# Every fourth partition: a block exchange of an attention and expert kernel laid out anew

## The chip, the cores and the metric

The kernel runs on one core of a Trainium2 chip. Its time is the device time of one launch in microseconds (us), from the start to the end of the program on that core; the figure to be compared is the median of several launches. All engines are named as in the profile: PE is TensorE (its weight loads are listed as PEld), DVE is VectorE, ACT is ScalarE, POOL is GpSimd, and SP is SyncE, which here only issues DMAs.

## What is computed

Sixteen sequences of 256 tokens with 256 features each go through an attention block and then, all 4096 tokens together, through a mixture of eight experts. All numbers are float32. Cut to what matters:

```python
h   = _ln(x, ln1_g, ln1_b) + silu(t) @ W_ada.T + b_ada
qkv = (h @ Wqkv.T).reshape(b, n, 3, H, HD)                 # H = 16 heads, HD = 64
q   = _ln(qkv[:, :, 0].transpose(0, 2, 1, 3), qn_g, qn_b)  # norm over HD
k   = _ln(qkv[:, :, 1].transpose(0, 2, 1, 3), kn_g, kn_b)
v   = qkv[:, :, 2].transpose(0, 2, 1, 3)
attn = softmax(einsum('bhnd,bhmd->bhnm', q, k) / sqrt(HD))
o   = einsum('bhnm,bhmd->bhnd', attn, v)
x   = x + o.transpose(0, 2, 1, 3).reshape(b, n, H * HD) @ Wout.T
tok = x.reshape(-1, d)
vals, idx = top_k(softmax(tok @ Wgate.T).T, bs // E)       # each expert takes 512 tokens
# then per expert: norm, fc1, gelu, fc2, times vals, added back to tok[idx]
```

The sum over a head's 64 columns, of which the norms of q and k need the mean and the squares, does not depend on the order of these columns. Neither does the product of q and k, as long as both have the same order. That is what the change makes use of.

## The kernel before

**Stages.** A short start loads weights and norms the first sequence. Then 16 sequences pass through attention, overlapped with each other; the trace has their norms' evictions (line 659) on average 47 us apart. From about 750 us on the last sequence, the choice of the experts' tokens and then 16 expert jobs follow (8 experts, in two halves), to the end at 1089.5 us.

**Order.** The kernel writes its own order. Every piece of work is a step with an engine and a place in time (`Plan`, line 45); the places are a fixed list of numbers (`PLACES`, line 182), sorted once. So each engine has a fixed queue, worked off in order, and an instruction that waits holds up all that stand behind it on its engine. The same holds for SP, whose queue of DMA issues is worked off in order too.

**One sequence.** For each of six groups of 512 columns of the weights `wq` (two for q, two for k, two for v) and each of the two halves of 128 tokens, `Group.matmul` (line 688) makes `pm`, 128 tokens by 512 columns, in PSUM. For q and k, ACT squares it (701), DVE sums the squares over each head (705), POOL makes the inverse root (711, 103), and DVE scales `pm` into `qk` in SBUF (721). The mean has been taken out of the weights beforehand, once (`center`, 600).

q and k are needed with the head's columns on partitions. For the first and the last sequence (`DIRECT`, line 171), TensorE turns them (730). For the other 14 the turn is an *exchange* in two parts. DVE's transpose (754) turns blocks of 32 by 32: afterwards partition 32k + d holds column d of a block for the tokens of block k. Then the four block rows have to change places with the four quarters of partitions, and that is done by DMA: `away` (761) stores all 128 partitions into a DRAM buffer `blocks[k, d, q, n]` (512 KB), and `back` (773) reads it with four loads of 128 KB, one for each quarter q of the columns, each into 32 partitions. ACT then applies gain and bias (`affine`, 781 and 789).

The softmax takes the same way. `Quad.scores` (813) puts scores of 128 tokens by 256 keys into PSUM banks (tile `sc`, four of them), DVE takes the maxima (821), ACT the exponentials with their sums (830, tile `pr`), DVE the inverse (837), POOL normalises (841), DVE turns 32 by 32 blocks (851), SP stores (859) and loads with four DMAs (873), and `product` (900) multiplies with v. `evict` (915), the output projection (926) and the routing's gate (963) end a sequence.

**Buffers that couple the engines.** `pm` and other small products share three PSUM banks of the tag `mm`; `sc` has four banks; `pb` (the turned blocks) three buffers, the DRAM blocks four, `prT` four.

Before the change, the load of quarter q writes the 32 partitions from 32q on. The order of the keys in the scores' columns is (block k, half t, m), and the exponentials are taken over 256 columns that lie side by side.

## Time and profile before

| What | Value |
|---|---|
| three runs | 1093.52, 1088.24, 1091.94 us |
| median | 1091.94 us |
| the profiled execution: its own time | 1091.3 us |
| its span, first to last instruction | 1089.5 us |
| granted TensorE clock, mean of the span | 0.993 |
| DMAs of the exchanges | 168 stores of 512 KB, 672 loads of 128 KB |
| all DMA traffic | 238.56 MB, of it 100.66 MB written to HBM |

The profile is a page and a trace of one execution. Its groups give, for all instructions of a line with the same operands, the count, the time in which any of them ran (busy), the mean duration of one in ns, and how long the engine stood idle just before them, with what ended that idle time. The table of stages gives the busy time of each engine in a stretch of the span, the granted clock, the mean busy share of the 16 DMA engines and the rate they moved. The table of waits names who waited, for whom, the total in us, how often and the longest wait. A busy TensorE need not be one at its peak, since the ends of matmuls are modelled; the distance from one start to the next is the firmer measure.

### The profile page before, as it was taken

Reading aid. Unit: us, or ns where it says so; the run is one execution under the profiler, and the core shown is the slowest. Engines: PE = TensorE matmul, PEld = TensorE weight load, DVE = VectorE, ACT = ScalarE, POOL = GpSimd, SP = SyncE. Lnnn points to the kernel's source line nnn. Section 1 sums busy time; section 2 is a strip of 40 time slices with the busy share of each in tenths; the row PEclk is TensorE's granted clock in tenths of the full one; section 3 lists DMA queues with packets and bytes.
Section 4 is the critical chain, followed back from the end, with each engine's and each line's share of the span. In section 5 each row is a group of like instructions: output and inputs, shape, how many; then the busy total and the mean of one; then the engine's idle time right before and its main releaser. Section 6 shows DMA issues by size and latency. Waiting matters only on the chain. (4 is left out here: it accounts for less than half of the span.)

```text
span 1089.5 us, 18716 instructions
## 1 busy us (share of the span) xinstructions
PE 1050.4 (96%) x5611; PEld 686.6 (63%) x5611; DVE 809.4 (74%) x2257; ACT 592.3 (54%) x1656; POOL 617.5 (57%) x997
## 2 busy tenths in 40 slices
PE   6999999999999999999999999999988999999996
PEld 4555646555454655555565555656667888888885
DVE  6658888889788797898888887885678588655440
ACT  1768666666566665675666656675612322332331
POOL 3676776778667686667757666665501333333332
PEclk9999999999999999999999999999999999999998
DMA  6025899999999999998999999985130556655661
GB/s 214 1 78 165 269 276 304 291 281 257 283 292 280 280 299 290 289 280 263 277 299 286 265 302 265 321 260 164 61 102 20 149 161 199 186 171 163 192 203 20
DMA packets 167700, 238.56 MB, mean 219 GB/s; under 512 B 17328, under 2 KB 139440, under 8 KB 167600
## 3 DMA queue, kind: packets, MB, share of 16 engines
q1 hardware_dynamic: 159680, 227.08, 69.9%
q0 software_dynamic: 6144, 8.39, 4.2%
q10 hardware_dynamic: 1776, 1.90, 0.5%
q8 instruction: 45, 0.74, 0.3%
q14 instruction: 55, 0.45, 0.1%
HBM read 136.64 MB, written 100.66 MB: 218 GB/s over the span
## 5 line engine op out<-in xcount | busy, mean ns | idle before, releaser
L688 PE MATMUL pm<-wq,hT 128*128 128x512 f32 x768 | 362.1, 607 | 10.1 <-DVE qk L721 3.9
L841 POOL TENSOR_SCALAR pr<-pr,sums 128x256 f32<-128x256 f32 x512 | 237.6, 485 | 102.6 <-DVE sums L837 95.0
L830 ACT ACTIVATE pr<-sc,nmax 128x256 f32<-128x256 f32 x512 | 237.7, 482 | 92.3 <-DVE nmax L821 75.2
L688 PEld LDWEIGHTS pm<-wq,hT 128*128 128x128 f32 x768 | 137.1, 191 | 165.3 <-issue 131.3
L103 POOL TENSOR_TENSOR ss<-ss,neghalf 128x8 f32<-128x8 f32 x128 | 211.2, 1650 | 10.7
L821 DVE TENSOR_REDUCE nmax<-sc 128x2 f32<-128x512 f32 x256 | 165.3, 672 | 19.4 <-PE sc L813 19.1
L851 DVE STREAM_TRANSPOSE pb<-pr 128x512 f32<-128x512 f32 x224 | 150.0, 689 | 15.9 <-POOL pr L841 9.4
L813 PE MATMUL sc<-kT,qT 64*128 64x256 f32 x1024 | 136.8, 396 | 1.0 <-ACT kT L789 0.6
L701 ACT ACTIVATE sq<-pm 128x512 f32<-128x512 f32 x128 | 76.4, 605 | 102.5 <-PE pm L688 100.5
L900 PE MATMUL po<-prT,v 128*64 128x256 f32 x1024 | 129.0, 387 | 1.3 <-DMA prT<-blocks 1.3
L813 PEld LDWEIGHTS sc<-kT,qT 64*128 64x128 f32 x1024 | 91.3, 186 | 50.3 <-issue 28.9
L1319 POOL DMA_INDIRECT out<-y,idx x32 | 51.3, 1604 | 120.6 <-DVE y L1313 66.0
L1286 PE MATMUL ph<-xT,w 128*128 128x256 f32 x512 | 117.8, 383 | 0.0
L1302 PE MATMUL py<-w,hid 128*128 128x256 f32 x512 | 116.3, 380 | 0.0
L926 PE MATMUL pw<-wo,oT 128*128 128x256 f32 x512 | 115.3, 382 | 0.0
L926 PEld LDWEIGHTS pw<-wo,oT 128*128 128x128 f32 x512 | 96.2, 190 | 20.9 <-issue 6.0
L830 ACT ACTIVATION_READ_ACCUMULATOR pr<-sc,nmax 128x1 f32 x512 | 109.2, 213 | 0.0
L900 PEld LDWEIGHTS po<-prT,v 128*64 128x64 f32 x1024 | 66.5, 136 | 66.0 <-issue 20.1
L705 DVE TENSOR_REDUCE ss<-sq 128x8 f32<-128x512 f32 x128 | 85.0, 669 | 28.8 <-ACT sq L701 28.3
L1293 ACT ACTIVATE hid<-ph,vec 128x256 f32<-128x256 f32 x128 | 60.4, 474 | 84.4 <-PE ph L1286 79.4
L1302 PEld LDWEIGHTS py<-w,hid 128*128 128x128 f32 x512 | 95.6, 190 | 12.8
L1286 PEld LDWEIGHTS ph<-xT,w 128*128 128x128 f32 x512 | 95.4, 190 | 12.8
(141 smaller groups left out, 1098.3 us busy)
## 6 DMA issues: line engine op xcount, KB each, us to landing
blocks<-pb SPq DMA_DIRECT2D x112, 512.0 KB, 4.7
prT<-blocks SPq DMA_DIRECT2D x448, 128.0 KB, 4.1
kblocks<-kb SPq DMA_DIRECT2D x56, 512.0 KB, 4.1
w<-in_fc2T SPq DMA_DIRECT2D x16, 1024.0 KB, 5.8
w<-in_fc1T SPq DMA_DIRECT2D x16, 1024.0 KB, 8.3
qraw<-kblocks SPq DMA_DIRECT2D x112, 128.0 KB, 4.0
kT<-kblocks SPq DMA_DIRECT2D x112, 128.0 KB, 4.1
out<-tok SPq DMA_DIRECT2D x32, 128.0 KB, 3.9
```

The lines of the kernel that those rows point to most:

```text
L103: nc.gpsimd.tensor_tensor(dst, src, neghalf[:, : src.shape[1]], ALU.pow)
L688: nc.tensor.matmul(self.pm, hTs[self.b][:, c, bass.ts(self.t, P)], wq[:, c, bass.ts(self.g, GW)], start=(c == 0), stop=(c == DC - 1),)
L705: nc.vector.tensor_reduce(self.ss[:, 0, :], self.sq.rearrange("p (h d) -> p h d", d=HD), AX.X, ALU.add,)
L813: nc.tensor.matmul(self.sc[i, j][:, t, :], qTs[self.b][rows, hp, bass.ts(t, P)], keys[rows, hp] if direct else keys[rows, hp // 4, hp % 4] ...
L821: nc.vector.tensor_reduce(self.nmax[i, j], self.sc[i, j], AX.X, ALU.max, negate=True)
L830: nc.scalar.activation(self.pr[i, j][:, t, :], self.sc[i, j][:, t, :], AF.Exp, bias=self.nmax[i, j][:, t : t + 1], scale=1.0, accum_out=se ...
L841: nc.gpsimd.tensor_scalar(self.pr[i, j][:, t, :], self.pr[i, j][:, t, :], self.sums[i][:, 1, j, t : t + 1], 1.0, ALU.mult, ALU.mult,)
L851: nc.vector.transpose(self.pb[i][:, :, :, j].rearrange("p k c t n -> p t k c n"), self.pr[i, j].rearrange("p t (k c m) -> p t k c m", c=TB ...
L900: nc.tensor.matmul(self.po[j * HD : (j + 1) * HD, i, :], vs[self.b][:, c, bass.ts(4 * self.d + 2 * i + j, HD)], prT[:, j, c] if self.b in ...
L926: nc.tensor.matmul(self.pw, oTs[self.b][:, hp // 2, self.t, hp % 2, :], wo[:, hp, :], start=(hp == 0), stop=(hp == HP - 1),)
L1286: nc.tensor.matmul(self.ph[f], self.w1[:, c, bass.ts(f, P)], self.xT[:, c, :], start=(c == 0), stop=(c == DC - 1),)
L1302: nc.tensor.matmul(self.py[i], self.hid[:, f, bass.ts(i, P)], self.w2[:, f, :], start=(f == 0), stop=(f == FC - 1),)
```

## The change

The 32 partitions that a load writes are no longer neighbours: the load of quarter q writes the partitions q, q + 4, q + 8 and so on. For that, column 4d + q of a pair of heads has to stand at place d of quarter q. The weights for q and k are therefore laid out on the host by quarter: a group's 512 columns stand as (quarter, head, 16 columns) where they stood as (head, 64 columns). All that goes by head on these columns (centering, sum of squares, scaling) now walks four runs of 16 columns for each head.

For the softmax the keys of the scores are now in their natural order, and the exponentials read each fourth column of PSUM and write 64 of them side by side, quarter after quarter. For the two sequences without an exchange, the scaling writes `qk` in the original order of columns, each element four elements from the last. The centering becomes three instructions where it was two.

```diff
         def center(g, c):
-            w3 = wq[:, c, bass.ts(g, GW)].rearrange("p (h d) -> p h d", d=HD)
+            w3 = wq[:, c, bass.ts(g, GW)].rearrange("p (q e d) -> p q e d", q=QB, e=8)
             ws = stat.tile([P, 8], F32, tag="ws", bufs=2, name="ws")
-            nc.vector.tensor_reduce(ws, w3, AX.X, ALU.add)
-            nc.vector.scalar_tensor_tensor(
-                w3, ws.unsqueeze(2).to_broadcast([P, 8, HD]), -1.0 / HD, w3, ALU.mult, ALU.add
-            )
+            nc.vector.tensor_reduce(ws, w3.rearrange("p q e d -> p e q d"), AX.XY, ALU.add)
+            nc.vector.tensor_scalar_mul(ws, ws, -1.0 / HD)
+            nc.vector.tensor_tensor(w3, w3, by_head(ws), ALU.add)
+
+        def by_head(x):
+            return x.unsqueeze(1).unsqueeze(3).to_broadcast([P, QB, 8, HD // QB])
...
                 nc.vector.tensor_reduce(
-                    self.ss[:, 0, :], self.sq.rearrange("p (h d) -> p h d", d=HD),
-                    AX.X, ALU.add,
+                    self.ss[:, 0, :], self.sq.rearrange("p (q e d) -> p e q d", q=QB, e=8),
+                    AX.XY, ALU.add,
                 )
...
+                if self.b in DIRECT:
+                    dst = self.qk.rearrange("p (e d q) -> p q e d", q=QB, e=8)
+                else:
+                    dst = self.qk.rearrange("p (q e d) -> p q e d", q=QB, e=8)
                 engine.tensor_tensor(
-                    self.qk.rearrange("p (h d) -> p h d", d=HD),
-                    src.rearrange("p (h d) -> p h d", d=HD),
-                    self.ss[:, 1, :].unsqueeze(2).to_broadcast([P, 8, HD]), ALU.mult,
+                    dst, src.rearrange("p (q e d) -> p q e d", q=QB, e=8),
+                    by_head(self.ss[:, 1, :]), ALU.mult,
                 )
...
                 nc.vector.transpose(
                     kb[0][:, :, self.t],
-                    self.qk.rearrange("p (h q d) -> p q h d", q=QB, d=SQ),
+                    self.qk.rearrange("p (q h d) -> p q h d", q=QB, d=SQ),
                 )
...
                     nc.sync.dma_start(
-                        raw[bass.ts(q, SQ)], self.blocks[:, :, q].rearrange("k d n -> d k n")
+                        raw[q::QB], self.blocks[:, :, q].rearrange("k d n -> d k n")
                     )
...
                 keys = plain(kTs[self.b]) if direct else (
-                    kTs[self.b].rearrange("p g k t h m -> p g h (k t) m")
+                    kTs[self.b].rearrange("p g k t h m -> p g h t k m")
                 )
...
                 for t in range(TB):
+                    dst, src = self.pr[i, j][:, t, :], self.sc[i, j][:, t, :]
+                    if not (self.b in DIRECT):
+                        dst = dst.rearrange("p (q c m) -> p q c m", q=QB, c=TB)
+                        src = src.rearrange("p (c m q) -> p q c m", q=QB, c=TB)
                     nc.scalar.activation(
-                        self.pr[i, j][:, t, :], self.sc[i, j][:, t, :], AF.Exp,
+                        dst, src, AF.Exp,
...
                     nc.sync.dma_start(
-                        prT[bass.ts(q, SQ)], self.blocks[i][:, :, q].rearrange("k m n -> m k n")
+                        prT[q::QB], self.blocks[i][:, :, q].rearrange("k m n -> m k n")
                     )
...
+    qk = a["Wqkv"][: 2 * H * HD].reshape(-1, 8, HD // 4, 4, D).transpose(0, 3, 1, 2, 4)
...
-        "wqkvT": a["Wqkv"].T,
+        "wqkvT": np.concatenate([qk.reshape(-1, D), a["Wqkv"][2 * H * HD :]]).T,
```

Each engine's queue has the same instructions in the same order as before, apart from eight small multiplications on DVE, one for each centering. The number of DMAs, their sizes and their order in SP's queue are the same.

## The prediction

> **What bounds the kernel now.** I read the engines' shares first, then the stages, the waits and the groups of the lines that the change touches. The page's busy lines, the stages of the exchange (75 to 735 us) and of the expert jobs (850 to 1080 us; columns: time, then PE, PEld, DVE, ACT and POOL busy with instructions, granted clock, DMA share, GB/s):

> ```profile
> PE 1050.4 (96%) x5611; PEld 686.6 (63%) x5611; DVE 809.4 (74%) x2257; ACT 592.3 (54%) x1656; POOL 617.5 (57%) x997
> DMA  6025899999999999998999999985130556655661
> ...
> 75.00:735.00 660.00, 650.80 (x3156) 368.00 (x3154) 553.40 (x1099) 435.66 (x1286) 456.81 (x786) 1.00 0.96 277
> 850.00:1080.00 230.00, 229.64 (x1486) 201.03 (x1484) 134.63 (x731) 73.65 (x151) 77.32 (x64) 1.00 0.58 170
> ```

> TensorE is the bound: 650.8 of 660 us in the exchange stage, at full clock. Since its ends are modelled I also took the distances between starts: a matmul of the groups starts 429 ns after the last in the median, scores 108 ns on average in the first sequence and in the exchanged ones alike, the projection 216 ns. These are the same at all times. Adding up what is beyond the usual distance for each pair of lines gives 24.7 us of real stalls between 60 and 800 us, and 14 us in the first 50. No more than these can be won by anything that leaves TensorE's work alone. Beside it the 16 DMA engines are 96% busy in the exchange stage (277 GB/s), DVE 84% (553.4 of 660), ACT 66%.

> Who waits for DMAs, and for DVE:

> ```profile
> ACT kT L789 <- DMA kT<-kblocks: 12.3, 13, 1.9
> DVE st L615 <- DMA xs<-in_x: 11.5, 6, 4.0
> ACT qT L781 <- DMA qraw<-kblocks: 8.9, 8, 3.0
> DVE pb L851 <- DMA kblocks<-kb: 5.0, 6, 2.0
> PE pm L688 <- DVE qk L721: 3.9, 4, 2.9
> ```

> (Waiter, what for, total us, times, longest.) The loads of the softmax's exchange hardly appear: the products start 6.3 us (median) after their operands have landed, and only one stalled, for 1.25 us. The DMAs are full, but TensorE mostly doesn't feel it.

> **The change part by part.**

> *Loads onto every fourth partition.* 672 loads of 128 KB; number, bytes and SP's issues stay. In the trace, the 79,650 packets of 1 KB between 150 and 700 us, three quarters of them of these loads, take 66.9 ns on average: 45% take 45 to 50 ns, 38% 70 to 110. In the expert stage such packets take 51.6 ns. If the slow ones are those that share a way into SBUF, and spreading them makes all like the expert stage's, the engines save 15.3 ns x 79,650 / 16 = 76 us each of 550: their share falls from 0.98 to 0.84, and loads land earlier than today's 4.0 to 4.1 us. What reaches TensorE is only what it now loses behind a DMA: I followed the larger stalls back and find five, of 1.42 (149.7 us, product on its own load), 1.48 (279.3, behind DVE's wait for `xs`), 0.62 (406.9), 0.85 (472.4) and 0.89 us (658.8), the last three behind ACT's waits for `kT` and `qraw`. The rest is hidden. That is 5.3 us; as some will only shrink I take **-5.0**. Bounds: 0, and all stalls, -24.7.

> [...]

> *Exponentials read each fourth column* (16 bytes apart), 448 of the 512:

> ```profile
> L830 ACT ACTIVATE pr<-sc,nmax 128x256 f32<-128x256 f32 x512 | 237.7, 482 | 92.3 <-DVE nmax L821 75.2 <-POOL pr L841 7.8 <-POOL ss L103 4.8
> L1172 DVE TENSOR_SCALAR partf<-pplace 128x256 f32<-128x256 f32 x2 | 0.8, 424 | 4.1 <-PE pplace L1161 4.1
> ...
> L998 DVE TENSOR_TENSOR gate_of<-gates,smax 128x224 f32<-128x224 f32 x1 | 0.8, 765 | 0.0
> L990 DVE TENSOR_TENSOR gates<-gates,smax 128x224 f32<-128x224 f32 x1 | 0.4, 391 | 0.0
> ```

> No row shows ACT or PSUM with such steps. L998 writes SBUF in steps of 128 bytes, L990 does the same work in a row: (765 - 391) / 224 = 1.67 ns more an element. L1172 writes in steps of 8 bytes: 424 ns, as much as rows of 256 elements written in a row take (411 to 424, L627), so free; L1173 beside it also reads so, at 422. So an exponential costs between +0 and 256 x 1.67 = +428 ns. It is a read in steps of 16 bytes, nearest to L1173's read: I take **0**. Priced as a rival below.

> [...]

> *Scaling.* 128 instructions of 512 elements, 678 ns (L721). 112 read and write in a row as before: 0. The 16 of the first and last sequence write in steps of 16 bytes: 0 to 512 x 1.67 = 855 ns each. Between 8 and 128 bytes neither row is near, so I take half, 0.43 us. In the first sequence TensorE waits for these very instructions (the 3.9 us above, 2.9 of them at 24 us), so eight count: **+3.4** (0 to +6.8). Those of the last lie in DVE's idle 16%; without that cover, 3.4 to 6.8 more.

> *Centering.* One tiny instruction more for each of eight: L837's 128x4 takes 157 ns and is the nearest, so 0.16 us each. The first two are hidden by the 2.0 us for which DVE then waits for the next weights; five lie between that and the scaling at 23.4 us for which TensorE waits: **+0.8**. Nothing hidden would be 1.3.

> *Sums of squares* read runs of 16 elements: L705 takes 669 ns with runs of 64 for each head, the maxima (L821) 672 with runs of 256. Run length shows no price; 0. *Turns:* L754 (four rows of runs) 695 ns, L851 (all in a row) 689: 112 x 6 ns = 0.7 us of DVE, hidden in its idle time. *Keys in natural order:* scores take 108 ns with keys in a row (first sequence) and in runs of 32 (the others); still runs of 32: 0. Weights laid out on the host cost the chip nothing.

> *Sum.* The profiled execution took 1091.3 us (span 1089.5 and 1.8 around it; the median of the runs is 0.6 above). 1091.3 - 5.0 + 3.4 + 0.8 = **1090.5 us**: no change that can be told. A measurement of this kernel tells about 0.5% (5.5 us) from none.

> **The rivals.**

> A, the sum above: reads are free, and the queue's relief is small. Bounds with its own terms: 1083 (twice the DMA's gain, scaling free) to 1097 (scaling at full price and some of it in the last sequence). Chance 0.43.

> B, slower: **the stepped read of PSUM costs ACT.** At the middle, +214 ns, a sequence's 32 exponentials add 6.8 us to ACT's 31 of every 47 us. I pushed each exponential in the trace back by that, let ACT's idle time take up what it can, and compared with the time that TensorE's waits on ACT had to spare (a new score finds its bank free 3 us early in the median, 1.0 in the tightest tenth): 41 waits come late, and the latest in each 6 us add up to 19 us. So 1110 us. It decides early: 4 us at +100 ns, 9 at +150, 44 at +300, 154 at +428. Squares that come late also keep DVE and the banks of `mm`, which is not in it. For it: L998; against it: L1172, and that L998 is a write. Chance 0.35, mostly 1097 to 1135.

> C, faster: **the full DMA queue is behind more stalls than I could follow** (DVE's and SP's waits for stores, slow issues). Half of the 24.7 us goes: 1091.3 - 12.4 + 0.8 = 1079.7 us. Against it: the 6.3 us that products have to spare. Chance 0.11.

> D, **the loads get no faster**, because the packets are slow for another reason (stores and loads mixed, HBM): then only costs are left, 1091.3 + 3.4 + 0.8 = 1095.5 us. For it: the spread of the packets between 70 and 110 ns isn't one sharp peak. Chance 0.11.

> **How the numbers follow.** The likeliest is A with 1090.5 us. Faster by over 0.5% (below 1086.5): 0.13 of A and C's 0.11, 0.24. Within: 0.26 of A, 0.08 of D, 0.02 of B, 0.36. Slower (above 1097.4): 0.33 of B, 0.04 of A, 0.03 of D, 0.40. For 8 in 10 the range reaches from C's value, 1079, to the better part of B, 1125; A alone would be 1083 to 1097.

> **What will show it.** The exponentials' mean: 482 ns, or 600 and more. The mean of the 1 KB packets, near 52 or still 67, and the DMA share of the exchange stage, 0.84 or 0.96. The waits of ACT for `kT` and `qraw` should halve. The sixteen scalings in steps, at 678 or up to 1530 ns. The stalls of TensorE in the exchange stage, 20 us or fewer under A, about 45 under B. I am wrong if an exponential costs 100 ns more, or if the stalls nearly vanish with the DMA's load.

## The result, and the profile after

The changed kernel takes 1128.82 us in the median of four runs (1125.81 to 1130.98); the kernel before, beside it on the same chip, 1090.55 us (four runs, 1088.24 to 1093.52). The ratio is 1.0347, with a 95% interval of 1.0307 to 1.0388: it is slower, and lies above the predicted range. The profiled execution has a span of 1124.0 us, against 1089.5.

First the same lines of the page and the stages as before (busy engines, DMA share in 40 slices; then time, PE, PEld, DVE, ACT, POOL busy, clock, DMA share, GB/s):

```profile
PE 1062.0 (94%) x5611; PEld 691.8 (62%) x5611; DVE 816.3 (73%) x2265; ACT 592.4 (53%) x1656; POOL 615.7 (55%) x997
DMA  6024878887877788787888877777221366566661
...
75.00:735.00 660.00, 631.57 (x3014) 356.73 (x3013) 531.59 (x1058) 413.49 (x1219) 437.97 (x756) 0.99 0.79 264
850.00:1080.00 230.00, 225.84 (x1517) 197.79 (x1516) 152.28 (x828) 72.82 (x153) 73.89 (x63) 0.99 0.54 159
```

In the exchange stage the DMA share is down from 0.96 to 0.79, and TensorE starts 3014 matmuls where it started 3156. The stage has 660 us, so TensorE is idle for 28 of them (660 - 631.57), where it was for 9. Less load on the DMAs came with less work done by all engines: 264 GB/s, where it was 277.

Who waits for DMAs, and for DVE (waiter, what for, total us, times, longest):

```profile
DVE st L617 <- DMA xs<-in_x: 19.2, 8, 5.4
DVE pb L860 <- DMA kblocks<-kb: 17.0, 11, 3.3
ACT qT L786 <- DMA qraw<-kblocks: 16.2, 10, 4.8
ACT kT L794 <- DMA kT<-kblocks: 14.2, 13, 2.0
PE pm L690 <- DVE qk L727: 9.6, 8, 3.9
```

Every one has grown: the waits for `qraw` from 8.9 us, for `kT` from 12.3, for a `pb` buffer that a store still holds from 5.0, for `xs` from 11.5, TensorE's for the scalings from 3.9. Yet the packets, the pieces of which a transfer consists, are not slower. Those of 1 KB between 150 and 700 us take 54.2 ns on average (66.9 before), 90% of them under 50. And the exponentials, the prediction's main fear, cost what they did (482 ns before):

```profile
L839 ACT ACTIVATE pr<-sc,nmax 128x256 f32<-128x256 f32 x512 | 237.1, 480 | 106.5 <-DVE nmax L826 84.9 <-POOL pr L850 9.9 <-PE po L909 4.9
```

What had changed is in the detail of one line, the loads of the softmax's exchange. The columns are the engine, the operation and its count, then the time that issuing one keeps SP busy (shortest/median/longest in ns), and the first and last start in us; the rest isn't used here. Before:

```profile
L873 SPq DMA_DIRECT2D prT<-blocks x448: 302/430/2175, 97.3 to 748.8; - x150
```

After:

```profile
L882 SPq DMA_DIRECT2D prT<-blocks x448: 577/602/1706, 100.0 to 781.8; - x150
```

A load onto every fourth partition takes SP 602 ns to issue instead of 430, and never less than 577. The loads of q and k show the same. The last one is issued 33.0 us later than before, which is nearly all of the 34.5 us by which the span grew. Summed over the exchange stage, SP is busy issuing DMAs for 523 us of 660, where it was 410. SP's own waits fit this: an engine that comes later finds more of what it waits for done. Before and then after, its waits for the softmax's stores to land (total us, times, longest):

```profile
SPq L873 <- DMA blocks<-pb: 63.4, 44, 5.5
```

```profile
SPq L882 <- DMA blocks<-pb: 29.3, 21, 3.6
```

The loads differ in the program as built, too. Every DMA that SP and ACT issue in the kernel before carries a mark, 979 in all. In the changed kernel 307 carry it; the 672 without it are the stepped loads. It is called the mark for a short issue here, since the loads of the kernel before, with nothing else changed, took 599 ns to issue without it (run 3). The trace agrees: in it SP's stores are still issued in 319 ns at the least, the stepped loads never under 577.

### The profile page after: what moved, and what is told of

Same layout as the page of the kernel before. It is cut to its first block, busy times and chain, and to the rows that moved or that the text cites. A ratio compares the mean times of both kernels' runs of the same rounds, so it can differ in the third digit from the quotient of the medians.

```text
span 1124.0 us, 18753 instructions
## 1 busy us (share of the span) xinstructions
PE 1062.0 (94%) x5611; PEld 691.8 (62%) x5611; DVE 816.3 (73%) x2265; ACT 592.4 (53%) x1656; POOL 615.7 (55%) x997
## 5 line engine op out<-in xcount | busy, mean ns | idle before, releaser
L690 PE MATMUL pm<-wq,hT 128*128 128x512 f32 x768 | 368.5, 616 | 16.7 <-DVE qk L727 9.6
L690 PEld LDWEIGHTS pm<-wq,hT 128*128 128x128 f32 x768 | 139.7, 194 | 174.4 <-issue 141.0
L103 POOL TENSOR_TENSOR ss<-ss,neghalf 128x8 f32<-128x8 f32 x128 | 210.5, 1645 | 10.6
L1328 POOL DMA_INDIRECT out<-y,idx x32 | 51.2, 1599 | 119.0 <-DVE y L1322 68.7
L727 DVE TENSOR_TENSOR qk<-pm,ss 128x512 f32<-128x512 f32 x128 | 93.2, 729 | 19.1 <-POOL ss L103 16.6
```

The source lines that it names most:

```text
L103: nc.gpsimd.tensor_tensor(dst, src, neghalf[:, : src.shape[1]], ALU.pow)
L690: nc.tensor.matmul(self.pm, hTs[self.b][:, c, bass.ts(self.t, P)], wq[:, c, bass.ts(self.g, GW)], start=(c == 0), stop=(c == DC - 1),)
L727: engine.tensor_tensor(dst, src.rearrange("p (q e d) -> p q e d", q=QB, e=8), by_head(self.ss[:, 1, :]), ALU.mult,)
```

## The experiments

Theory 1: SP's dearer issues make the loss. Theory 2: the rest of the change makes it (scalings, centering, exponentials). Theory 3: a load that steps over partitions lands late by itself. Twelve kernels were run:

| Kernel | median us | ratio to before, 95% interval | 1 KB packet, ns | load issue, median ns |
|---|---|---|---|---|
| the change | 1128.82 | 1.0347 (1.0307 to 1.0388) | 54.2 | 602 |
| 1 only the loads | 1123.68 | 1.0310 (1.0281 to 1.0338) | 53.6 | 603 |
| 2 all but the loads | 1094.95 | 1.0038 (1.0020 to 1.0056) | 67.4 | 430 |
| 3 old loads, dear issue | 1122.37 | 1.0293 (1.0260 to 1.0326) | 58.4 | 599 |
| 4 one load per exchange | 1082.19 | 0.9924 (0.9897 to 0.9952) | 51.2 | 374 |
| 5 only the scalings | 1093.11 | 1.0014 (0.9999 to 1.0029) | 66.1 | 430 |
| 6 only the centering | 1093.29 | 1.0013 (0.9999 to 1.0027) | 66.3 | 430 |
| 7 as 4, gathered scalings | 1079.92 | 0.9883 (0.9863 to 0.9903) | 51.9 | 374 |
| 8 dear issue, softmax only | 1113.98 | 1.0198 (1.0171 to 1.0224) | 61.5 | 599 |
| 9 four loads by k | 1083.51 | 0.9931 (0.9908 to 0.9954) | 52.9 | 432 |
| 10 as 4, dear issue | 1081.48 | 0.9912 (0.9882 to 0.9942) | 51.3 | 586 |
| 11 unpadded blocks | 1098.76 | 1.0069 (1.0043 to 1.0095) | 67.9 | 430 |
| 12 spread only | 1081.34 | 0.9920 (0.9904 to 0.9935) | 52.9 | 430 |

The kernel before was run again with each group, at 1089.56 us (1 to 4), 1092.45 (5 to 8), 1090.89 (9, 10), 1091.61 (11) and 1090.56 (12); so ratios are compared, not medians of different groups. The expected times of runs 5 to 8 stand on the first group's 1089.56. Packets are means between 150 and 700 us, issues those of the softmax's loads.

**Which part of the change.** Run 1, the kernel before with:

```diff
-    raw[bass.ts(q, SQ)], self.blocks[:, :, q].rearrange("k d n -> d k n")
+    raw[q::QB], self.blocks[:, :, q].rearrange("k d n -> d k n")
...
-    prT[bass.ts(q, SQ)], self.blocks[i][:, :, q].rearrange("k m n -> m k n")
+    prT[q::QB], self.blocks[i][:, :, q].rearrange("k m n -> m k n")
```

> The kernel before with one edit: the 672 exchange loads write every fourth partition (rows of q, k and the softmax blocks then stand in another order, so the output is not the reference's). Theory 1 (SP issues a stepped load in 602 ns instead of 430, SP falls behind, buffers come late): about 1120 to 1125 us, 1 KB packets near 54 ns as in the changed kernel, loads issued in 577 to 602 ns, SP's waits for stores about halved. Theory 2 (the loads are harmless, the direct scalings, the centering and the stepped exponentials cost the time): 1085 to 1092 us. Theory 3 (a load that steps over partitions lands later by itself): 1120 to 1125 us too; this run does not tell 3 from 1.

Run 2 is the changed kernel with the same lines turned back.

> The changed kernel with the 672 loads put back on 32 neighbouring partitions (output not the reference's). Theories 1 and 3: what is left is the 16 dearer direct scalings and the centering, 1092 to 1097 us, loads issued in 302 to 430 ns, 1 KB packets near 67 ns. Theory 2: 1120 us or more.

The loads alone lose 3.1%, everything else together 0.4%. Theory 2 falls. The stages of the two (run 1, then run 2) agree: with the old loads the DMA share is at 0.96 again and TensorE at 651 us.

```profile
75.00:735.00 660.00, 631.25 (x3006) 355.57 (x3005) 531.34 (x1058) 412.28 (x1218) 436.90 (x755) 0.99 0.79 264
```

```profile
75.00:735.00 660.00, 650.87 (x3149) 368.10 (x3148) 554.55 (x1095) 434.71 (x1282) 456.67 (x786) 1.00 0.96 276
```

**Issue or partitions.** Run 3 leaves every partition of the kernel before as it was and takes away the mark alone, around the four loads of both `back` functions:

```diff
+    nc.dge_precook = False
     for q in range(QB):
         nc.sync.dma_start(
...
+    nc.dge_precook = True
```

> The kernel before, every byte and every partition as it was, but the 672 loads are built without the flag that marks a DMA as prepared for a short issue, as the changed kernel's loads lack it. Theory 1: loads issued in 577 to 602 ns, 1 KB packets still near 67 ns, and 1120 to 1130 us, no less than with the stepped loads, because the packets are not faster here. Theory 3: the issue is not what counts, 1089 to 1095 us. Theory 2: 1089 to 1095 us as well.

The softmax's loads in its trace, and its exchange stage:

```profile
L876 SPq DMA_DIRECT2D prT<-blocks x448: 555/599/1690, 96.7 to 780.7; - x150
```

```profile
75.00:735.00 660.00, 632.83 (x3004) 357.88 (x3003) 531.32 (x1058) 412.82 (x1219) 437.97 (x755) 0.98 0.83 264
```

With 32 neighbouring partitions as before and an issue of 599 ns, the whole loss is there: 1.0293, against 1.0310 with the stepped loads, within each other's intervals. Theory 3 isn't needed. One could still ask whether a load without the mark also lands late, since the traces record no landings where such loads occur. Each DMA of SP ends in 16 packets of 4 bytes (15,552 for 972 DMAs in each of these traces), and if the DMAs are taken to end in their order, these give an estimate of when. By it a softmax load ends 2.5 us after the start of its issue in the change and 2.6 in run 3, against 3.0 before (where the recorded landing is 4.1), so no later.

One expectation missed: the packets were to stay near 67 ns, and they took 58.4, with a DMA share of 0.83; with two thirds of the loads dear (run 8) they took 61.5. So a good part of the faster packets in the changed kernel need not come from the partitions. That loads which are issued more slowly are less in each other's way is one reading; no run tests it.

**More or fewer dear issues.** Run 8 makes only the 448 loads of the softmax dear, run 10 the loads of run 4.

> The kernel before with only the 448 softmax loads built without the short issue; the 224 loads of q and k keep it. Theory 1 in proportion to SP's added time: 1089.6 + 32.8 x 448 / 672 = 1111.5 us, say 1106 to 1116. If only what exceeds SP's capacity in a sequence counts (a queue that fills up late), clearly less: 1092 to 1104 us.

Two thirds of the dear issues give 2.0% of the 2.9%, in proportion. Run 4 uses what the new layout makes possible. Partition 4d + q takes row (d, q) of the DRAM block, so that for each k the rows of all 128 partitions stand in DRAM in one run once the padding row is left out, and a single load can take them all:

```diff
-    for q in range(QB):
-        nc.sync.dma_start(
-            prT[q::QB], self.blocks[i][:, :, q].rearrange("k m n -> m k n")
-        )
+    nc.sync.dma_start(prT, self.blocks[i].rearrange("k m q n -> (m q) k n"))
...
-    self.blocks[i] = dram.tile([QB, SQ, QB + 1, N], F32, tag="blocks", bufs=4, name="blocks")
+    self.blocks[i] = dram.tile([QB, SQ, QB, N], F32, tag="blocks", bufs=4, name="blocks")
```

(and the same for q and k).

> The changed kernel with each exchange's four stepped loads replaced by one load of all 128 partitions (512 KB; the DRAM blocks without their padding row, so that d and q are one run of rows). 168 loads in place of 672, and all of them carry the flag for the short issue. Theory 1: SP's work for loads falls from 672 x 0.6 = 403 us to 168 x 0.3 to 0.6 = 50 to 100 us, its waits for stores grow, and the time falls below the changed kernel's by at least its whole loss, to 1075 to 1095 us. If an issue costs by the rows it describes (four times as many), 4 x 0.43 us, the time is near the kernel before, 1090 to 1100 us. Theories 2 and 3 (the loss lies in the layout or in the landing, not in the issues): 1115 to 1130 us.

> The kernel with one load per exchange (1082.19 us), its 168 loads built without the short issue. If each dear issue costs the kernel the same wherever it stands (32.8 us / 672 = 0.049 us each): 168 x 0.049 = 8 us more, 1090 us. If dear issues cost only because SP's queue was full, and a quarter of the loads leaves it slack: 1082 to 1085 us.

The load lines of run 4 and of run 10:

```profile
L878 SPq DMA_DIRECT2D prT<-blocks x112: 359/374/1160, 99.9 to 736.8; - x112
```

```profile
L881 SPq DMA_DIRECT2D prT<-blocks x112: 579/586/1173, 99.9 to 735.6; - x112
```

Run 4 is faster than both kernels. Run 10 issues each load at 586 ns and loses nothing to it: SP then issues for 198 us of the 660 instead of 170, and has idle time enough to take that up. A dear issue cost this kernel time where SP's queue was well filled (410 us of 660 before, 518 in run 3), and none where it was not. About 170 ns more of SP's time for each load of 128 KB (599 ns against 430) were worth 2.9% (run 3). Issues from another engine's queue weren't tried.

**What the packets are worth.** Run 4 changed two things at once, the number of issues and the partitions that a load covers. Run 9 keeps four loads with the short issue, each filling a quarter of all 128 partitions:

```diff
-    nc.sync.dma_start(prT, self.blocks[i].rearrange("k m q n -> (m q) k n"))
+    for k in range(QB):
+        nc.sync.dma_start(prT[:, k], self.blocks[i][k].rearrange("m q n -> (m q) n"))
```

> The changed kernel with each exchange's four loads cut by k instead of by q: each load fills one quarter of every one of the 128 partitions (128 rows of 1 KB), from DRAM blocks without the padding row. 672 loads as before, all with the short issue as before: the case that was foreseen in the prediction, faster packets at unchanged issues. Packets near 51 ns as with one load per exchange, issues 302 to 430 ns. Against the 1094.95 us of the changed kernel with the old loads: if the 12.8 us that one load per exchange brought come from the packets, 1082 to 1084 us; if they come from SP's relief, 1093 to 1096 us; if the prediction's term of 5.0 us for the packets was right, near 1090 us.

It keeps nearly all of run 4's gain, so that gain is not SP's relief. But run 9 also reads DRAM in one run, without the padding. Run 11 takes only the padding from the kernel before, and run 12 keeps the DRAM side exactly as it was and lands each load on all partitions:

```diff
-    prT[bass.ts(q, SQ)], self.blocks[i][:, :, q].rearrange("k m n -> m k n")
+    prT[:, q], self.blocks[i][:, :, q].rearrange("k m n -> (k m) n")
```

> The kernel before with one edit: its DRAM blocks lose their padding row (a row of blocks is 4 KB behind the next instead of 5 KB), which the kernels with one load and with four loads by k also lost. If the gain of those two comes from where a load lands in SBUF (all 128 partitions instead of 32), nothing changes: 1088 to 1093 us, 1 KB packets near 67 ns. If it came from the missing padding: 1077 to 1084 us, packets near 52 ns. If the padding was there for the reads: slower than 1095 us, packets above 70 ns.

> The kernel before with one edit: each of the 672 loads reads the same 128 rows of 1 KB from the same padded DRAM blocks as before, but lands them on all 128 partitions, one row each, instead of four rows on each of 32 neighbours (so rows stand in other places and the output is not the reference's). Same number and order of loads, short issues, layout and scalings of before. This is the prediction's term for faster packets by itself. If spreading over the partitions makes packets fast and that is what the four loads by k won: packets near 53 ns, 1077 to 1082 us. If that gain came from reading DRAM in one run: packets near 67 ns, 1088 to 1093 us. If the prediction's 5.0 us were right: 1085 to 1087 us.

Without the padding the kernel before gets slower, with packets as before and stores that land in 4.9 us instead of 4.7. Spreading alone gives 0.8%. In the list of DMA issues (size of one, median us from issue to landing) the loads of the kernel before, and then of run 12:

```profile
prT<-blocks SPq DMA_DIRECT2D x448, 128.0 KB, 4.1
...
kT<-kblocks SPq DMA_DIRECT2D x112, 128.0 KB, 4.1
```

```profile
prT<-blocks SPq DMA_DIRECT2D x448, 128.0 KB, 3.3
...
kT<-kblocks SPq DMA_DIRECT2D x112, 128.0 KB, 3.3
```

The loads land 0.8 us earlier, and ACT's waits for `kT` and `qraw`, 12.3 and 8.9 us before, are down to 3.2 and 1.3. TensorE's idle time in the exchange stage falls from 9.2 to 2.0 us. This is the nearest that a run comes to the prediction's first term by itself: spread over all partitions, though not over every fourth, with the issue kept cheap.

**The small terms.** Runs 5 and 6 make only the stepped writes of the scalings, and only the new centering.

```diff
-    self.qk.rearrange("p (h d) -> p h d", d=HD),
+    self.qk.rearrange("p (e d q) -> p q e d", q=QB, e=8),
```

> The kernel before with one edit: the 16 direct scalings write in steps of 16 bytes, as in the changed kernel (the columns of q and k of the two direct sequences then stand in another order, so the output is not the reference's). Scalings near 1.09 us each. If they and the centering are what is left without the loads (1094.95 against 1089.56 us), the scalings alone give most of it: 1092 to 1095 us; if they lie beside other work, 1089 to 1091 us.

> The kernel before with one edit: the weights of q and k are centered by reduction over two axes, a small multiplication and an addition, over columns by quarter (the weights still stand by head, so the wrong columns are averaged together; the output is not the reference's). By the rows of the changed kernel 8 multiplications of 0.17 us are all that is added: 1089.5 to 1091.5 us. If more, the start of the kernel waits for the centered weights longer than its rows say.

Run 5's 16 stepped scalings beside its 112 others, then run 7's, which read PSUM in steps and write their row of SBUF in order:

```profile
L728 DVE TENSOR_TENSOR qk<-pm,ss 128x512 f32<-128x512 f32 x112 | 75.9, 679 | 15.8 <-POOL ss L103 14.3
L722 DVE TENSOR_TENSOR qk<-pm,ss 128x512 f32<-128x512 f32 x16 | 17.5, 1096 | 2.8 <-POOL ss L103 2.4 <-PE pq L737 0.4
```

```profile
L724 DVE TENSOR_TENSOR qk<-pm,ss 128x512 f32<-128x512 f32 x16 | 10.9, 683 | 5.5 <-PE pq L739 3.0 <-POOL ss L103 2.4
```

```diff
-    dst = self.qk.rearrange("p (e d q) -> p q e d", q=QB, e=8)
+    nc.vector.tensor_tensor(
+        self.qk.rearrange("p (e d q) -> p e d q", q=QB, e=8),
+        src.rearrange("p (q e d) -> p e d q", q=QB, e=8),
```

> The kernel with one load per exchange (1082.19 us), with the 16 direct scalings turned round: they read PSUM in steps and write their row of SBUF in order, where before they read in order and wrote in steps of 16 bytes. If a stepped PSUM read costs VectorE nothing, as it costs ScalarE nothing in the exponentials: scalings near 0.70 us and 1077 to 1080 us. If it costs as much as the stepped write: 1.09 us and no change, 1081 to 1083 us.

Each of runs 5 and 6 costs about 0.14%, 1.5 us, and neither is told from nothing by itself; together with whatever else remains they give run 2's 0.4%. Run 7 is the fastest of all: 1079.92 us against 1092.45 beside it, 1.2% under the kernel before. In its exchange stage the DMAs move more than before, 281 GB/s, at a share of 0.83, and TensorE starts 3221 matmuls where it started 3156:

```profile
75.00:735.00 660.00, 659.98 (x3221) 377.66 (x3220) 562.38 (x1117) 440.95 (x1306) 468.36 (x807) 1.00 0.83 281
```

## Why the prediction was wrong

**The step that failed** is the first sentence on the loads: "number, bytes and SP's issues stay". Number and bytes did; the issues went from 430 to 602 ns, and this term, counted as nothing, is the loss. Run 3 measures it alone: 2.9%, or 1089.56 x 0.0293 = 31.9 us. With run 2's 0.4% (4.1 us) it makes 3.3%, inside the interval of the change. Two facts could be had before the run: that the stepped loads lack the mark stands in the program as built, and how full SP was, 410 of 660 us, could be summed from the trace of before. What an issue without the mark costs could not, as all of SP's and ACT's carry it there. Why a stepped load is built without it no run shows. 672 x 0.17 us is 114 us more for an engine that works its queue off in order (its 972 issues start in the program's order in both traces); 28% of it reached the end.

**How it reaches TensorE.** No wait for SP is among the large ones, because SP's lateness appears as waits for DMAs. Those of run 3, where only the issue differs from before, are the ones that grew in the change:

```profile
DVE st L615 <- DMA xs<-in_x: 21.8, 8, 5.2
ACT qT L783 <- DMA qraw<-kblocks: 19.7, 10, 3.8
DVE pb L853 <- DMA kblocks<-kb: 17.3, 12, 3.1
ACT kT L791 <- DMA kT<-kblocks: 17.1, 15, 2.5
```

In run 10, with fewer dear issues and loads that cover all partitions, what is left of them:

```profile
DVE st L617 <- DMA xs<-in_x: 4.8, 2, 3.8
...
ACT qT L785 <- DMA qraw<-kblocks: 1.7, 1, 1.7
DVE tn L629 <- DMA kblocks<-kb: 1.0, 1, 1.0
```

The waits for `xs` are loads of the next inputs that stand behind the exchange's in SP's queue, and those for `kblocks` are DVE waiting until a store that SP issued late has read its `pb` buffer. So TensorE is fed late from three sides, and no one tile shows the loss.

The waits are not the whole loss. From 75 us to the issue of the last softmax load, before and after, TensorE does the same work:

```profile
75.00:748.80 673.80, 664.60 (x3224) 377.53 (x3222) 561.89 (x1118) 441.15 (x1306) 467.20 (x806) 1.00 0.95 276
```

```profile
75.00:781.80 706.80, 676.18 (x3225) 382.62 (x3224) 565.29 (x1120) 442.23 (x1307) 467.32 (x808) 0.99 0.79 263
```

Of the 33.0 us more, 21.4 are idle time of TensorE (30.6 against 9.2) and 11.6 are matmuls that take longer. A part of these goes with the granted clock (the third column from the right). In this stretch of the change it stood at 0.50 three times, 17 us in all, and before not once; rows from within each of the three:

```profile
389.70:392.90 3.20, 3.20 (x12) 2.01 (x12) 2.83 (x6) 3.04 (x11) 0.00 (x0) 0.50 0.65 198
440.90:447.50 6.60, 6.60 (x13) 3.38 (x13) 2.35 (x8) 4.21 (x16) 2.77 (x6) 0.50 0.90 319
741.20:747.90 6.70, 6.46 (x18) 3.17 (x20) 6.07 (x11) 4.77 (x13) 3.88 (x6) 0.50 0.73 223
```

Each began within 1 us of the end of an idle time of TensorE of 1.6 to 2.9 us. In them a matmul of the groups starts 854 ns after the last in the median, in the rest of the stretch 429. Half the clock for 17 us delays its work by at most 8.5 us, an estimate. In run 3 the clock stood at 0.50 for 20.4 us between 75 and 735. So part of the loss is a slower clock that went with the stalls, not the stalls themselves; no run separates the two.

**The packets' term, -5.0,** had the direction right and the size too small. Spread over all partitions at an unchanged issue, packets take 52.9 ns (run 12), near the 52 foreseen. Whether the slower ones share a way into SBUF, as the estimate supposed, no run shows. The spreading is worth 0.8% (0.65 to 0.96), 8.7 us, in run 12. Of the five stalls that I had followed to a DMA I allowed 5.0 us; more hung on it, which was rival C's thought. In the changed kernel this gain does not show: runs 1 and 3, with stepped and with neighbouring partitions, take the same time. Either the gain is hidden behind SP's lateness, or stepping has a cost of its own as large; no run separates these. And the falling DMA share, which the prediction named as a sign for A, also appears in run 3, where no partition was touched.

**The exponentials at 0** were right: 480 ns with steps of 16 bytes in PSUM. Rival B's mechanism, and its price, are out. That its 1110 us lies nearer to the result than the forecast is chance, and the upper bound of the range, taken from it, still missed the result by 4 us.

**Scaling and centering,** +3.4 and +0.8: a stepped scaling costs 0.42 us (1096 - 679 ns), where the half price was 0.43. What reached the end was about 1.5 us of the 3.4 (run 5, -0.1 to 3.2) and 1.4 of the centering (run 6, -0.1 to 2.9). The 2.9 us of both and the forecast 4.2 both lie within run 2's interval (2.2 to 6.1 us). Run 7, which takes the stepped writes out of run 4's kernel, gains 0.4% on it (0.9883 against 0.9924, with intervals that overlap), so 3.4 us for the scalings is not ruled out.

**Sums of squares, turns and keys at 0** were right: the sums take 671 ns (669 before), the turns 696 and 688 (695 and 689), and run 2, which has the new order of keys, starts the matmuls of the scores 109 ns apart on average (110 before). Rival D is out by run 12, where the packets got faster at the same issues.

**Slips that decide nothing.** Of the packets of 1 KB that the prediction counts, nine in ten are of the exchange's loads (558 loads of 128 packets each between 150 and 700 us), not three quarters. And C's sum leaves out the 3.4 us for the scalings that A and D have. A's lower bound comes to 1082.1 us by its own terms, not 1083.

## What to carry to other kernels

When a change alters the shape of a DMA, compare how the DMA is built and what its issue costs the engine that issues it, and multiply by the issues; here a queue worked off in order and 62% busy passed 28% of the added time on to the end. A falling DMA share is no proof of relief: it falls as well when the transfers are only asked for more slowly (0.83 in run 3, from 0.96). A layout that puts source and destination rows into the same order paid here only where it let one whole-tile DMA (run 4), or loads over all partitions (run 9), take the place of four on 32.
